# Head-sized TensorE tiles for the attention products of a two-layer convolution kernel, with the scaling on ScalarE

## The chip, the core and the metric

The kernel runs on one core of one Trainium2 chip, in one launch. The metric is the device time of the whole launch in microseconds (us). Shares and stages below come from one profiled execution of the kernel before the change.

## What is computed

The input holds 32 images of 1024 channels and 14 x 14 = 196 positions, in 32-bit floats. Layer 0 is a chain of three table look-ups by soft assignment, with normalisations between them; the change does not touch it. Layer 1 is a linear attention with 16 heads of 64 channels and a depthwise 3 x 3 convolution beside it:

```python
q = elu(Wq @ x[:, :512] + bq) + 1          # 1024 features per position
k = elu(Wk @ x[:, 512:] + bk) + 1
q_rope, k_rope = rope(q), rope(k)          # rotation of feature pairs
z = 1 / (einsum('bhdn,bhd->bhn', q, mean_n(k)) + 1e-6)
kv = (1 / n) * einsum('bhdn,bhen->bhde', k_rope, v)   # v = x, by heads, n = 196
out = einsum('bhdn,bhde->bhne', q_rope, kv) * z
x = x + out + depthwise3x3(x)              # x inside is group-normalised
```

Each head has its own 64 x 64 matrix `kv`. Products of one head's keys with another head's values are not part of the result.

## The kernel before, in words

The launch has two parts. Layer 0 fills the first 2310 us or so. Layer 1 follows; it takes the images two at a time, in 16 pairs, and `pair(p, t)` writes down the work of pair `p`.

In layer 1 nothing is issued in program order. Every piece of work is handed to `do(engine, rank, weight, fn, reads, writes, ...)`. `Plan.write()` then runs a small simulation with the pieces' weights (microseconds) as durations and the ranks as priorities, and issues the pieces of each engine in the order in which the simulation starts them. So each engine's instruction order is fixed when the kernel is built, and an engine that waits for one piece does not take the next one. The ranks of pair `p` are those of the table `due`, shifted by 80 per pair, so that work of neighbouring pairs interleaves.

The work of one pair, by the names and lines that matter below:

- **Front** (`front`, L1623 to L1642): finishes layer 0 for this pair; ScalarE scales (L1623), VectorE adds and takes statistics (L1632, L1637, L1642). `group_norm` averages them with small TensorE products (L1679) and ends on GpSimd. `normalise` (L1736) writes the normalised image `y` with a margin, and a scaled copy `x`.
- **Projections** (`channels`, L1770 to L1791): 16 pieces, each of four 128 x 128 x 392 TensorE products into a bank of the ring `mm`, then two ScalarE steps (L1779, L1782) and one VectorE step (L1787 for queries, L1791 for keys).
- **Rotation** (`rope`, L1814, L1815): on GpSimd.
- **Token-major copies** (`tokens`, L1832, L1835): TensorE transposes four blocks into an `mm` bank, ScalarE copies them out into `vt` (values) or `kt` (keys). The positions of an image are cut in two halves of 105.
- **Key-value products** (`products`, L1856 to L1895): four pieces per pair, one for each image `i` and each half `jp` of the features. A piece has 16 matmuls (two feature tiles `j`, real and imaginary part `r`, two position halves `h`, two column halves `hp`). One of them has 105 rows, 64 weight columns and 128 moving columns, so it covers two heads' keys against two heads' values, and half of what it computes belongs to no head. VectorE's `blocks` (L1878) multiplies the 128 x 512 result by the mask `bmask`, which zeroes the foreign blocks and holds the factor 1/196 too, and writes the tile `kv`.
- **Normalisers** (`normalisers`, L1902 to L1930): 16 matmuls of 128 rows and 32 weight columns, each feature tile into its own 32 output partitions (L1920), then a VectorE reciprocal (L1930). `normalise_q` (L1955) multiplies the rotated queries on GpSimd.
- **Query products** (`attend`, L1974): four pieces per pair, one per feature tile. A piece has eight matmuls (two images, `r`, two halves `hp` of the rows) of 64 rows and 128 weight columns; rows 0 to 63 go to the PSUM bank `pa[0]`, rows 64 to 127 to the bank `pa[1]`.
- **Convolution** (`lepe`, L1992): VectorE adds seven or eight of the nine taps onto the `pa` banks, one instruction per tap, and adds the sum to `x` (L2006). Further taps go over ScalarE and GpSimd (`side_tap`, L2021, L2029). In the last pair three of four feature tiles have their taps as diagonal matmuls on TensorE instead (L2048).

PSUM is shared out as four `mm` banks, three `pa` banks and one bank `w`. A bank of `mm` is taken by any of the projections, transposes, products and normalisers, and is free again when its reader is done. There is one `kv` tile for each `i` and `jp`, so that a pair's result can be written only after the query products of the pair before have read theirs.

`tables` makes the mask once, with two VectorE instructions (L476, L477), during layer 0. A multiplication of 32-bit numbers shows as two TensorE passes in the trace: every matmul leaves two matmul records and two weight-load records.

Of the kernel before, what the change touches and what calls it, by code (L numbers as in the profile page):

```python
# [11 lines left out]
AF = mybir.ActivationFunctionType  # L12
ALU = mybir.AluOpType
# [4 lines left out]
P = 128  # L18
C = 1024
CT = C // P  # L20
HW = 196
# [11 lines left out]
def bc(ap, axis, n):  # L33

    u = ap.unsqueeze(axis)
    shape = list(u.shape)
    shape[axis] = n
    return u.to_broadcast(shape)
# [12 lines left out]
class Plan:  # L51
# [13 lines left out]
    def do(self, engine, rank, weight, fn, reads=(), writes=(), port=False, lag=0.12):  # L65
        n = len(self.pieces)
        before = set()
        for k in reads:
            before |= {self.last[k]} if k in self.last else set()
            self.read.setdefault(k, []).append(n)  # L70
        for k in writes:
            before |= set(self.read.pop(k, []))
            before |= {self.last[k]} if k in self.last else set()
            self.last[k] = n
        slots = []
        for k in (*reads, *writes):
            s = k[0] if isinstance(k, tuple) else k
            if isinstance(s, Slot) and s not in slots:
                slots.append(s)
                s.left += 1  # L80
        self.pieces.append((engine, rank, weight, fn, before - {n}, slots, port, lag))
# [68 lines left out]
def conv_preact_kernel(ctx: ExitStack, tc: tile.TileContext, a: dict, out: bass.AP):  # L150
    nc = tc.nc
# [272 lines left out]
    given = {}  # L424

    def attention_inputs(stack):

        def loads(_):  # L430
            pool = stack.enter_context(tc.tile_pool(name="pre", bufs=1, side="right"))

            def tile_(name, shape):
                given[name] = pool.tile(shape, F32, tag=name, name=name)
                return given[name]

            for n, k in (("qb", a["qb"]), ("kb", a["kb"].rearrange("o (r j p) -> p (o r) j", p=P, r=2))):
                nc.sync.dma_start(tile_(n, [P, 2, 4]), k)
                tile_(n + "u", [P, 2, 4])
                tile_(n + "d", [P, 2, 4])  # L440
            for n, shape in (("lepe_w", [P, CT, 9]), ("lepe_b", [P, CT]), ("kvmask", [P, 256])):
                nc.sync.dma_start(tile_(n, shape), a[n])

            for n in ("cosq", "sinq"):
                t = tile_(n, [P, 4, 14])
                v = a[n].rearrange("p j (r c) -> p j r c", c=14)
                nc.sync.dma_start(t[:, :2], v[:, :2, :, 0])
                nc.sync.dma_start(t[:, 2:], v[:, 2:, 0, :])
            for n, shape in (
                ("hmean", [P, 4]),  # L450
                ("bmask", [P, P]),
                ("hp", [P, 4, 32]),
                ("hsel", [P, P]),
                ("x1", [P, 4, N2]),
                ("x0", [P, 4, N2]),
                ("o3_0", [P, 2, N2]),
                ("o3_1", [P, 2, N2]),
            ):
                tile_(n, shape)
            for h in (1, 0):  # L460
                for i in range(2):
                    nc.sync.dma_start(
                        given[f"x{h}"][:, :, i * HW : (i + 1) * HW],
                        x[i, 4 * h * P : 4 * (h + 1) * P].rearrange("(c q) n -> q c n", q=P),
                    )

        def tables(scratch):
            g = given

            for n in ("qb", "kb"):  # L470
                nc.vector.tensor_scalar(g[n + "u"], g[n], 1.0, None, ALU.add)
                nc.vector.tensor_scalar(g[n + "d"], g[n], -1.0, None, ALU.mult)

            hmask = g["kvmask"].rearrange("p (h e) -> p h e", e=64)[:, :, 0]
            nc.vector.tensor_scalar(g["hmean"], hmask, 1.0 / HW, None, ALU.mult)
            nc.vector.tensor_tensor(g["bmask"], g["kvmask"][:, :P], g["kvmask"][:, P:], ALU.add)  # L476
            nc.vector.tensor_scalar(g["bmask"], g["bmask"], 1.0 / HW, None, ALU.mult)  # L477

            nc.vector.memset(g["hp"], 0.0)
            nc.vector.tensor_copy(g["hp"][:, :, :4], bc(hmask, 1, 4))  # L480

        def heads(scratch):
            g = given
            ph = scratch(P)
            nc.tensor.transpose(ph, g["hp"].rearrange("p j h -> p (j h)"), ident)
            nc.vector.tensor_copy(g["hsel"], ph)

        def third(_):
            for k in range(2):
                nc.sync.dma_start(given[f"o3_{k}"], o3d[:, 4 + 2 * k : 6 + 2 * k, :N2])  # L490

        def projection(b):
            t = a["wkT" if b < 4 else "wqT"]
            return lambda: load_lut(b, t[(b % 4) * P : (b % 4 + 1) * P])

        return [loads, third, tables, heads], [projection(b) for b in range(8)], [third]


# [977 lines left out]
    with ExitStack() as s:  # L1476
# [5 lines left out]

        wk, wq = weights[:4], weights[4:]
        bias = {n: (given[n + "u"], given[n + "d"]) for n in ("qb", "kb")}
        lw, lb, hmean, bmask, sel, cos, sin = (
            given[n] for n in ("lepe_w", "lepe_b", "hmean", "bmask", "hsel", "cosq", "sinq")
        )


# [6 lines left out]
        for k in range(2):  # L1496
            t = once.tile([P, CT, LY], F32, tag=f"y{k}", name=f"y{k}")
            v = t[:, :, LEAD : LEAD + 2 * IMG]
# [21 lines left out]
        for j in range(4):  # L1520
            t = once.tile([P, 2, 2, 2, TP], F32, tag=f"kr{j}", name=f"kr{j}")
# [14 lines left out]
        def ring(name, n, shape, pool=None, tag=None):  # L1536
            tiles[name] = [
                (pool or p2).tile(shape, F32, tag=tag or f"{name}_{k}", name=f"{name}_{k}")
                for k in range(n)
            ]  # L1540
# [11 lines left out]
            ring(f"kt{h}", 1, [TP, 2, 512])  # L1552
        for i in range(2):
            for jp in range(2):
                ring(f"kv{i}{jp}", 1, [P, 2, 2, P])
        for n, k in (("mm", 4), ("pa", 3), ("w", 1)):
            ring(n, k, [P, 512], mm)
        plan = Plan(tiles)
        do = plan.do
# [296 lines left out]
        def products(i, jp, kts, vts, rank):  # L1856

            pk = Slot("mm")
            t = Slot(f"kv{i}{jp}")

            def piece():
                pv = pk().rearrange("p (j r e) -> p j r e", j=2, r=2)
                for j in range(2):
                    for r in range(2):
                        for h in range(2):
                            for hp in range(2):
                                c = 2 * (2 * jp + j) + hp
                                k0 = (2 * j + r) * P + 64 * hp
                                nc.tensor.matmul(  # L1869
                                    pv[64 * hp : 64 * hp + 64, j, r],  # L1870
                                    kts[h]()[:, jp, k0 : k0 + 64],
                                    vts[h]()[:, c * P : (c + 1) * P],
                                    start=(h == 0),
                                    stop=(h == 1),
                                )

            def blocks():
                nc.vector.tensor_tensor(  # L1878
                    t().rearrange("p j r e -> p (j r) e"),
                    pk().rearrange("p (j e) -> p j e", e=P),  # L1880
                    bc(bmask, 1, 4),
                    ALU.mult,
                )

            do(
                PE,
                rank,
                1.97,
                piece,
                [(kt, jp) for kt in kts] + [(vt, jp) for vt in vts],  # L1890
                [pk],
                lag=0.25,
            )
            do(DVE, rank - 10, 0.61, blocks, [pk], [t])
            return t  # L1895

        def normalisers(p, qs, ks, rank):
# [66 lines left out]
        def attend(j, kvs, qr, pa, rank, onto):  # L1964

            def piece():
                for i in range(2):
                    for r in range(2):  # L1970
                        for hp in range(2):
                            v = slice(64 * hp, 64 * hp + 64)
                            n = 210 - 14 * i
                            nc.tensor.matmul(  # L1974
                                pa[hp]()[:, i * 210 : i * 210 + n],
                                kvs[i, j // 2]()[v, j % 2, r],
                                qr()[v, r, i * HW : i * HW + n],
                                start=(r == 0 and not onto),
                                stop=(r == 1 and (i == 1 or not onto)),
                            )  # L1980

            do(PE, rank, 1.57, piece, [kvs[0, j // 2], kvs[1, j // 2], qr], pa, lag=0.25)
# [277 lines left out]
```

## Time and profile before

| what | value |
|---|---|
| median of 3 runs | 3439.27 us (3438.05 to 3441.15) |
| profiled execution, its own time | 3446.09 us |
| its span in the trace | 3444.3 us |
| granted TensorE clock over the span | 0.99 |
| matmul records, busy time | 19217, 3368.4 us |
| VectorE busy, ScalarE busy, GpSimd busy | 2938.9, 1671.0, 2538.4 us |
| key-value products (L1869) | 2048 records, first 2368.3 us, last 3406.3 us |
| query products (L1974) | 1024 records, first 2398.2 us |

The profiled execution is 6.8 us longer than the median. In the profile, PE is the matmul side of TensorE and PEld its weight loads, DVE is VectorE, ACT ScalarE, POOL GpSimd, SP the engine that issues DMAs. "out<-in" names the tiles of a group of instructions. Durations of neighbouring instructions overlap a little, matmuls most of all, so the cost of a piece is read from its start to the start of the next one.

### The profile page before, as it was taken

The numbers are of one execution on the slowest core, as the hardware profiler recorded it, in microseconds if no ns is written. First come the engines' busy times: TensorE is split into PE (matmuls) and PEld (weight loads), VectorE is DVE, ScalarE is ACT, GpSimd is POOL, SyncE is SP. The second block draws the span as 40 slices with busy tenths as digits, with TensorE's granted clock in tenths as the row PEclk, the third lists the DMA queues.
The fourth block names the chain that finished last, engine by engine and source line by source line (L and its number), as shares of the span: only waits on it lengthen the run. The fifth ranks groups of instructions, "written<-read, shape, count | busy, mean of one in ns | idle before, by whom it ended". The sixth has DMA issues, their size and how long they took to land. (4 is left out here: it accounts for less than half of the span.)

```text
span 3444.3 us, 54933 instructions
## 1 busy us (share of the span) xinstructions
PE 3368.4 (98%) x19217; PEld 2088.5 (61%) x19217; DVE 2938.9 (85%) x4621; ACT 1671.0 (49%) x3843; POOL 2538.4 (74%) x1558
## 2 busy tenths in 40 slices
PE   8999999998999999999999999979999999999999
PEld 4555555554455445545488888866666666666665
DVE  7999999997888888888576666646999999999996
ACT  4555555554444434443311111118676767676765
POOL 5999999996888988898322222218888888888887
PEclk9999999999999999999999999989999999999999
DMA  3110111103434444443131111131233332333221
GB/s 117 46 48 28 46 46 47 30 24 113 134 109 128 123 114 109 127 123 98 33 91 38 49 49 49 47 130 41 69 90 87 87 87 81 87 87 91 79 76 48
DMA packets 242229, 267.44 MB, mean 78 GB/s; under 512 B 32812, under 2 KB 239700, under 8 KB 241944
## 3 DMA queue, kind: packets, MB, share of 16 engines
q1 hardware_dynamic: 241248, 263.52, 26.3%
q8 instruction: 155, 2.54, 0.3%
q14 instruction: 130, 1.06, 0.1%
q10 hardware_dynamic: 696, 0.31, 0.0%
HBM read 171.01 MB, written 77.09 MB: 72 GB/s over the span
## 5 line engine op out<-in xcount | busy, mean ns | idle before, releaser
L618 POOL TENSOR_TENSOR t<-t,r 128x1568 f32<-128x1568 f32 (+3 forms) x288 | 961.5, 3339 | 531.5 <-issue 201.1
L734 PE MATMUL po<-t,lut 128*128 128x392 f32 x3840 | 1334.6, 500 | 2.5 <-DMA t<-spare 2.5
L734 PEld LDWEIGHTS po<-t,lut 128*128 128x128 f32 x3840 | 711.9, 190 | 603.8 <-issue 83.2
L1770 PE MATMUL mm<-y,lut 128*128 128x392 f32 x2048 | 710.4, 493 | 0.1
L580 DVE STREAM_TRANSPOSE tt<-t 128x1568 f32<-128x1568 f32 (+1 forms) x284 | 517.8, 1823 | 153.4 <-ACT t L568 149.1
L568 ACT ACTIVATE t<-sc,cbias 128x392 f32<-128x392 f32 (+1 forms) x624 | 322.4, 598 | 554.5 <-PE sc L897 191.2
L1992 DVE SCALAR_TENSOR_TENSOR pa<-y,lepe_w,pa 128x406 f32<-128x406 f32 x900 | 537.9, 638 | 3.6 <-PE pa L1974 0.3
L611 DVE STREAM_TRANSPOSE r<-rc 128x1568 f32<-128x1568 f32 (+1 forms) x284 | 520.9, 1834 | 10.4
L1770 PEld LDWEIGHTS mm<-y,lut 128*128 128x128 f32 x2048 | 370.4, 188 | 243.1 <-issue 6.1
L583 POOL TENSOR_TENSOR tt<-tt 128x784 f32<-128x784 f32 x256 | 470.6, 1838 | 30.5 <-DVE tt L580 25.9
L568 ACT ACTIVATE t<-sc,room 128x392 f32<-128x392 f32 x512 | 259.1, 589 | 410.2 <-issue 180.1
L1358 PE MATMUL po<-t,lut 128*128 128x224 f32 (+2 forms) x1352 | 314.8, 416 | 1.3 <-DMA o3d<-o 1.3
L599 DVE TENSOR_REDUCE sm<-tt 128x98 f32<-128x784 f32 (+1 forms) x284 | 293.6, 1034 | 1.1 <-POOL tt L583 0.8
L1358 PEld LDWEIGHTS po<-t,lut 128*128 128x128 f32 (+1 forms) x1352 | 234.7, 190 | 64.5 <-issue 61.8
L601 DVE RECIPROCAL rc<-sm 128x98 f32<-128x98 f32 (+1 forms) x284 | 220.2, 775 | 9.8
L622 ACT ACTIVATE sm<-sm 128x98 f32<-128x98 f32 (+1 forms) x284 | 85.5, 301 | 150.5 <-DVE rc L601 150.5
L1623 ACT ACTIVATE w<-x,tb,gn_a 128x196 f32<-128x196 f32 x248 | 128.3, 517 | 53.8 <-DMA qr<-o3d 29.3
L1814 POOL TENSOR_TENSOR kr<-k,cosq 128x784 f32<-128x784 f32 x64 | 104.3, 1629 | 63.5 <-DVE k L1791 36.7
L1955 POOL TENSOR_TENSOR qr<-qr,zb 128x784 f32<-128x784 f32 x64 | 117.9, 1854 | 39.2 <-DMA zb<-zd 31.5
L1779 ACT ACTIVATE e<-mm,kbd 128x392 f32<-128x392 f32 x128 | 74.5, 582 | 145.4 <-PE mm L1770 145.4
L1782 ACT ACTIVATE e<-e 128x392 f32<-128x392 f32 x256 | 134.9, 527 | 2.1
L1736 ACT ACTIVATE y<-x,gb,ga 128x196 f32<-128x196 f32 x256 | 125.3, 544 | 12.1 <-POOL gb L1699 12.1
(215 smaller groups left out, 4613.1 us busy)
## 6 DMA issues: line engine op xcount, KB each, us to landing
patch<-h1d SPq DMA_DIRECT2D x383, 108.5 KB
x<-in_x_dram SPq DMA_DIRECT2D x32, 784.0 KB
o3d<-o SPq DMA_DIRECT2D x56, 448.0 KB
x<-in_x_dram SPq DMA_DIRECT2D x64, 392.0 KB
out_dram<-x SPq DMA_DIRECT2D x64, 392.0 KB
o<-o3d SPq DMA_DIRECT2D x62, 392.0 KB
h1d<-pad SPq DMA_DIRECT2D x96, 225.0 KB
patch<-h1d SPq DMA_DIRECT2D x383, 54.2 KB
```

Of the source, the lines that this page charges most:

```text
L568: nc.scalar.activation(t[:, j, : sc.shape[1]], sc, AF.Identity if exact else AF.Exp, bias=bias[:, j : j + 1],)
L580: nc.vector.transpose(tt, tf)
L583: nc.gpsimd.tensor_tensor(tv[:, :, :8], tv[:, :, :8], tv[:, :, 8:], ALU.add)
L599: nc.vector.tensor_reduce(sm, tv, AX.X, ALU.add)
L601: nc.vector.reciprocal(rc, sm)
L611: nc.vector.transpose(r, bc(rc, 2, KC))
L618: nc.gpsimd.tensor_tensor(v[:, c], v[:, c], r[:, c], ALU.mult)
L734: nc.tensor.matmul(po[h], luts[b][:, j, h * P : (h + 1) * P], ts[u % len(ts)][:, j, :N2], start=(b == 0 and j == j0), stop=(b == 7 and j = ...
L1358: nc.tensor.matmul(dst, w, x, start=start, stop=stop)
L1770: nc.tensor.matmul(pv(), w[kt][:, m0 : m0 + P], ywin(p, first + kt), start=(kt == 0), stop=(kt == 3),)
L1782: nc.scalar.activation(e(), e(), AF.Exp, scale=-1.0)
L1992: nc.vector.scalar_tensor_tensor(acc, neighbours(p, c, offset(k)), lw[:, c, k : k + 1], acc, ALU.mult, ALU.add,)
```

## The change

The products are cut along the heads. A feature tile of 128 rows holds four heads with 32 rows each (for one `r`), and each head meets 64 value columns.

- `products` issues 32 matmuls of 105 rows, 32 weight columns and 64 moving columns in place of 16 of 105 x 64 x 128. Four neighbouring ones write to the four 32-partition strips of the bank. The result has 256 columns in place of 512 and holds no foreign blocks.
- The mask and its two instructions are gone. `scaled`, one ScalarE instruction over 128 x 256, copies the result out of PSUM with the factor 1/196; it stands in for the VectorE instruction over 128 x 512.
- `attend` issues 16 matmuls of 32 rows and 64 weight columns in place of eight of 64 x 128. The rows of heads 0 and 1 go to partitions 0 to 63 and 64 to 127 of the bank `pa[0]`, those of heads 2 and 3 to the same halves of `pa[1]`.
- The planner's weights change with it: 1.2 in place of 1.97 for a product piece, and 0.42 on ScalarE in place of 0.61 on VectorE. The weight of `attend` stays at 1.57.

```diff
-            nc.vector.tensor_tensor(g["bmask"], g["kvmask"][:, :P], g["kvmask"][:, P:], ALU.add)
-            nc.vector.tensor_scalar(g["bmask"], g["bmask"], 1.0 / HW, None, ALU.mult)
...
-                ring(f"kv{i}{jp}", 1, [P, 2, 2, P])
+                ring(f"kv{i}{jp}", 1, [P, 2, 2, 64])
...
-                pv = pk().rearrange("p (j r e) -> p j r e", j=2, r=2)
+                pv = pk()[:, :256].rearrange("p (j r e) -> p j r e", j=2, r=2)
                 for j in range(2):
                     for r in range(2):
                         for h in range(2):
-                            for hp in range(2):
-                                c = 2 * (2 * jp + j) + hp
-                                k0 = (2 * j + r) * P + 64 * hp
+                            for q in range(4):
+                                c0 = (2 * (2 * jp + j)) * P + 64 * q
+                                k0 = (2 * j + r) * P + 32 * q
                                 nc.tensor.matmul(
-                                    pv[64 * hp : 64 * hp + 64, j, r],
-                                    kts[h]()[:, jp, k0 : k0 + 64],
-                                    vts[h]()[:, c * P : (c + 1) * P],
+                                    pv[32 * q : 32 * q + 32, j, r],
+                                    kts[h]()[:, jp, k0 : k0 + 32],
+                                    vts[h]()[:, c0 : c0 + 64],
                                     start=(h == 0),
                                     stop=(h == 1),
                                 )
 
-            def blocks():
-                nc.vector.tensor_tensor(
-                    t().rearrange("p j r e -> p (j r) e"),
-                    pk().rearrange("p (j e) -> p j e", e=P),
-                    bc(bmask, 1, 4),
-                    ALU.mult,
+            def scaled():
+                nc.scalar.activation(
+                    t().rearrange("p j r e -> p (j r e)"),
+                    pk()[:, :256],
+                    AF.Copy,
+                    scale=1.0 / HW,
                 )
...
-                1.97,
+                1.2,
...
-            do(DVE, rank - 10, 0.61, blocks, [pk], [t])
+            do(ACT, rank - 10, 0.42, scaled, [pk], [t])
...
-                        for hp in range(2):
-                            v = slice(64 * hp, 64 * hp + 64)
+                        for h in range(4):
+                            v = slice(32 * h, 32 * h + 32)
                             n = 210 - 14 * i
+                            e = slice(64 * (h % 2), 64 * (h % 2) + 64)
                             nc.tensor.matmul(
-                                pa[hp]()[:, i * 210 : i * 210 + n],
+                                pa[h // 2]()[e, i * 210 : i * 210 + n],
                                 kvs[i, j // 2]()[v, j % 2, r],
                                 qr()[v, r, i * HW : i * HW + n],
```

More of the change, by code (lines that the diff above doesn't have):

```diff
@@ L450, in loads @@
                 ("hmean", [P, 4]),
-                ("bmask", [P, P]),
                 ("hp", [P, 4, 32]),
@@ L1484, in conv_preact_kernel @@
         bias = {n: (given[n + "u"], given[n + "d"]) for n in ("qb", "kb")}
-        lw, lb, hmean, bmask, sel, cos, sin = (
-            given[n] for n in ("lepe_w", "lepe_b", "hmean", "bmask", "hsel", "cosq", "sinq")
+        lw, lb, hmean, sel, cos, sin = (
+            given[n] for n in ("lepe_w", "lepe_b", "hmean", "hsel", "cosq", "sinq")
         )
```

## The prediction

> **What bounds the kernel now.** I began with the page's busy shares, but they average two layers, and the change lies in the second. So I cut out a stretch there in which the pairs repeat. In the chain of waits the same steps return every 68.4 us; 2429.12 to 3181.90 us holds 11 such periods of 68.43 us. The view of busy time by stretch says of it:
>
> ```profile
> core 0: us, PE busy (x) PEld busy (x) DVE busy (x) ACT busy (x) POOL busy (x), PEclk, DMA share, GB/s
> 2429.12:3181.90 752.78, 745.96 (x4750) 504.56 (x4749) 735.88 (x1762) 525.84 (x1098) 633.04 (x571) 1.00 0.31 85
> ```
>
> PE is idle for 752.78 - 745.96 = 6.82 us, 0.62 us per period. DVE is idle for 16.90 us, 1.54 us per period. So TensorE works 67.8 us of each 68.43 and VectorE 66.9: **two engines are nearly full at once**. ScalarE works 47.8 us and GpSimd 57.5; they have room. A gain needs both PE and DVE to get less work, and this change takes from both.
>
> The chain of waits for one period confirms it. It runs through DVE and ACT for the first part and then along PE without a break:
>
> ```profile
> 2702.90 3.85 DVE pa L1992 x7
> ...
> 2711.78 1.77 ACT x L1736 x4
> ...
> 2718.82 1.17 PE mm L1832 x8
> 2719.98 2.64 PE mm L1770 x8
> 2722.62 1.90 PE mm L1869 x32
> 2724.52 0.61 PE mm L1832 x4
> 2725.13 2.64 PE mm L1770 x8
> 2727.77 1.90 PE mm L1869 x32
> 2729.66 5.47 PE mm L1770 x16
> ```
>
> Two of the pair's four product pieces (L1869) stand on the chain. The timeline of PE shows the other two and the pieces around them; the cost of a piece is the distance from its start to the next start:
>
> ```profile
> 2777.20 3.71 PE L1869 MATMUL mm<-vt,kt 105*64 105x128 f32 x64
> 2780.85 1.53 PE L1920 MATMUL mm<-q,kmm 128*32 128x196 f32 x32
> 2782.31 1.12 PE L1832 MATMUL mm<-ident,kr 128*105 128x128 f32 x8
> 2783.36 1.65 PE L1974 MATMUL pa<-qr,kv 64*128 64x210 f32 x16
> ```
>
> Two products together cost 3.65 us, one alone 1.90 (chain), so products take 2 x 1.90 + 3.65 = 7.45 us per pair. The normalisers cost 1.46 us and a query piece 1.57 (2735.41 to 2736.98 in the same view). The view of one line adds the VectorE step that goes:
>
> ```profile
> L1878 DVE TENSOR_TENSOR kv<-mm,bmask x64: 628/682/693, 2370.4 to 3407.6; 128x512 f32<-128x512 f32 x64
> L476 DVE TENSOR_TENSOR bmask<-kvmask x1: 283/283/283, 1806.5 to 1806.5; 128x128 f32<-128x128 f32 x1
> L477 DVE TENSOR_SCALAR bmask<-bmask x1: 226/226/226, 1806.8 to 1806.8; 128x128 f32<-128x128 f32 x1
> ```
>
> **What the Trainium skill says, and the trace.** (1) "TensorE: Matmul & The Clock Gate", section "The mechanism": matmuls in different tiles of the array run at the same time, with starts about 4 ns apart. The trace agrees on the overlap: in the products two records start 6.7 ns apart and the next two follow 109 ns later; in the normalisers four records start 6.7 ns apart, the next four 166 ns later; in layer 0 (L1027, 27 x 32 tiles) sixteen start within 100 ns. The weight loads of different tiles overlap in the same way. (2) The same page, section "Wait — 56ns, not 53.3ns?": a matmul of N columns costs N / 2.4 GHz + about 2.5 ns. A pass of a 32-bit matmul moves two cycles per column here: 128 x 2 / 2.4 + 2.5 = 109.2 and 196 x 2 / 2.4 + 2.5 = 165.8, and the trace has 109 and 166. The section also gives a floor of about 25 ns between starts of small matmuls; no stretch of this trace comes to it, since the densest sustained one, the normalisers, has 1464 / 32 = 45.8 ns per record. (3) "TensorEngine Tiling (Array Packing)", section "Key Properties": a change of the tiling mode drains the array. A product piece is 16 groups x 109.1 = 1.75 us, and costs 1.90, so such a change costs about 0.15 us. (4) "PSUM — Partial Sum Buffer", section "PSUM bank collisions raise a hardware error": it quotes that different row tiles cannot access one bank at the same time, and reports as measured that only the same bank and the same 32-partition strip collide. The changed `attend` puts two row tiles into two halves of one bank; no row of this trace does that, as each row tile there has a bank of its own.
>
> **The change, part by part, per pair.**
>
> *Products on PE.* 32 matmuls leave 64 records. Four neighbouring ones have four column strips, as in the normalisers, so 16 groups of four. A group streams 64 columns: 64 x 2 / 2.4 + 2.5 = 55.8 ns. Four starts at 6.7 ns need 27 ns, less than that. A load of 32 columns must fit behind a group: two loads of one strip start 28 ns apart in the normalisers. So a piece costs 16 x 55.8 + 0.15 = 1.04 us alone and two together 32 x 55.8 + 0.15 = 1.94: in all 4.02 us, a **saving of 3.43 us**. From below the bound is no drain at all, 0.89 us a piece. From above I take the normalisers' 45.8 ns per record, in case TensorE cannot be fed faster than shown: 64 x 45.8 = 2.93 us, dearer than now by 1.03. I take 1.04, since the sixteen starts of L1027 within 100 ns show that issue itself is quick.
>
> *Query products.* Before, eight groups of two records (four (image, r) steps, two passes); after, eight groups of four. The columns stay at 210 and 196, so the groups stay at 178 and 166 ns, and the cost at 1.57 us. A gain is possible: the first weight load has 64 columns, not 128, worth at most 0.05 us a piece. From above: if two row tiles of one bank take turns, each group streams twice, 8 x 172 = 1.38 us more per piece. I take no change.
>
> *VectorE.* Four L1878 go. From one start to the next they cost 0.60 us, so **2.39 us less**. L476 and L477 lie in layer 0, where PE is full from 1800 to 2200 us; their 0.5 us is worth nothing, and 0.5 us if that cover were gone.
>
> *ScalarE.* Four steps over 128 x 256 from PSUM come in. The copies of 512 columns (L1835) cost 0.47 us from start to start, the 392-column step L1779 0.48; I take 0.46, so 1.84 us more on an engine with 20 us idle per pair. Its own wait is the danger: ScalarE takes its pieces in order, and behind the step stand L1779 and L1782, for which VectorE (L1787, L1791) waits, and the copies L1835, for which PE waits. The planner starts it only when product and `kv` tile are ready in its own time, and the mask has the same waits on VectorE today, so I price it at zero; late by half a product piece four times would be 2 us per pair. No DMA is added or moved; POOL's and SP's instructions stay.
>
> *Order.* The new weights shift the simulated times by 3 of about 70 us and so reorder neighbours. I can't price this from the trace; see the rivals.
>
> **Sum.** PE: 67.81 - 3.43 = 64.4 us of work per pair. DVE: 66.89 - 2.39 = 64.5. They end level. A period of 64.5 plus DVE's present idle of 1.54 is 66.0, a gain of 2.4 us, and PE's idle grows from 0.6 to 1.6. Between the first and the last pair lie 15 periods: 36 us. In the tail the chain runs over two joined products (3.64 us, at 3324.78), worth 1.7 more. So 3446.1 - 37.7 = 3408.4 for an execution like the profiled one, which is 6.8 us above the median: **3401.6**. If DVE's idle shrinks to PE's 0.6, the gain is 3.3 a period, 3388; if it doubles, 0.9 a period, 3424. That is this case's own range.
>
> **The rivals.**
>
> *Row tiles of one bank take turns* (slower). `attend` then costs 1.57 + 1.38 = 2.95 us. PE has 64.4 + 4 x 1.38 = 69.9 us of work, with 0.6 idle 70.5, 2.1 above now: 15 x 2.1, plus 5.5 in the last pair, less 1.7, gives 3474. It decides from 1.57 + 3.43 / 4 = 2.43 us per piece on. For it speaks the quoted rule; against it the measured one on the same page, and row tiles with separate banks that overlap in L1974 and L897.
>
> *TensorE is not fed fast enough.* At the page's 25 ns per record a product piece costs 64 x 25 + 150 ns = 1.75 us, a saving of only 0.15 to 0.3: PE has 67.1 us, the period is 67.8, and the time about 3429. At 45.8 ns PE works 67.8 + 4 x 1.03 = 71.9 and the time is 3500. It turns to a loss above 1.90 us a piece.
>
> *The order eats it.* With ScalarE's step in front of its other work, or neighbours reordered, DVE's idle grows by the 2.4 us freed: 3437, no change. For it speaks that the two engines already wait on each other in turn along the chain; against it, that PE today idles only 0.6 us in the same coupling.
>
> **Chances.** Main case 0.63 (3402); slow feeding at 25 ns 0.09 (3429); order 0.09 (3437, half of it within the bound); turns in a bank 0.11 (3474); feeding at 45.8 ns 0.08 (3500). About 0.2%, 7 us, is what a measurement of this kernel can tell from no change. Faster by more: 0.63 + 0.09 less a little, 0.71; within: 0.09, the rest of main, feeding and order; slower: 0.20. The range runs from 3380, below the main case's best, to 3474, the centre of the next case; about 0.18 is left out.
>
> **What would show it.** L1869 with 4096 records, groups of four 56 ns apart, a lone piece about 1.04 us; L1974 with 2048 records, a piece still 1.57; L1878 gone from VectorE and a ScalarE row of 128 x 256 at about 0.5 us; the period 66.0 us, PE and DVE both idle by about 1.6. A query piece over 2.43 us, or a lone product over 1.90, would prove the forecast wrong on PE; a period of 68.4 with both pieces as forecast would prove the order wrong.

## The result, and the profile after

The changed kernel takes 3404.33 us (median of four runs, 3403.06 to 3404.95) against 3439.22 us before: a ratio of **0.9898**, 95% interval 0.988 to 0.9915, so 34.9 us faster. The forecast was 3401.6 us. The profiled execution took 3404.36 us (span 3402.6), 41.7 us less than the one before; 6.8 us of that is that the earlier one lay above its median.

Busy time by stretch of the changed kernel, over the 11 periods from the second pair's normalisers on:

```profile
core 0: us, PE busy (x) PEld busy (x) DVE busy (x) ACT busy (x) POOL busy (x), PEclk, DMA share, GB/s
2433.63:3157.80 724.17, 709.46 (x6861) 459.97 (x6860) 713.04 (x1715) 538.24 (x1141) 630.61 (x572) 1.00 0.31 89
```

724.17 us for 11 pairs are 65.8 us each, where it was 68.43. PE idles 14.7 us in the stretch (1.3 per pair; before 0.6) and DVE 11.1 (1.0 per pair; before 1.5). Both are still nearly full; there is less for them to do.

The chain of waits of the changed kernel, at the place where the prediction showed two product pieces of 1.90 us:

```profile
2699.55 2.15 PE mm L1829 x16
2701.70 2.70 PE mm L1767 x8
2704.40 1.03 PE mm L1866 x64
2705.43 0.61 PE mm L1829 x4
2706.05 2.64 PE mm L1767 x8
2708.68 1.03 PE mm L1866 x64
2709.71 2.83 PE mm L1767 x8
2712.54 1.53 PE pa L1972 x32
```

The product pieces (now L1866) cost 1.03 us with twice the records, and a query piece (L1972) 1.53 with twice the records. Two joined pieces stand in PE's timeline of the changed kernel:

```profile
2757.72 1.99 PE L1866 MATMUL mm<-vt,kt 105*32 105x64 f32 x128
2759.65 0.68 PE L1829 MATMUL mm<-ident,kr 128*105 128x128 f32 x4
```

From start to start the joined pair costs 1.93 us, where it was 3.65. The view of one line shows the step that took the mask's place:

```profile
L1875 ACT ACTIVATE kv<-mm x64: 359/366/396, 2367.7 to 3369.9; 128x256 f32<-128x256 f32 x64
```

Two things must be known to read the experiments. **Layer 0**, which no kernel here changes, ends (first L1623, in the changed kernel L1620) anywhere between 2296 and 2303 us from one profiled execution to the next. So I read each trace from that first step to the end, called *layer 1* below. And **the planner's order depends on a draw at each build**: it goes through a set of engine names, and the sequence in a set of names changes with each build. It matters in one place: the planner has a lock, `port`, that one engine holds at a time, and VectorE (one small step, L1902) and GpSimd can both want it at the same simulated moment. There are just two possible issue orders, and each trace could be matched, TensorE piece by piece, with one of the two: the kernel before had GpSimd first, the changed kernel VectorE first. The comparison above therefore mixes the change with the draw; the runs e9 and e10 take them apart. The kernel before that ran beside the experiments took 3447 to 3449 us, which fits VectorE first (e10 stands at 0.9999 of it, and e7, with GpSimd first, at 0.998).

| kernel | port first | median us | ratio (interval) | layer 1 us | period us | PE work + idle | DVE work + idle |
|---|---|---|---|---|---|---|---|
| before (first trace) | GpSimd | 3439.2 | 1 | 1142.4 | 68.50 | 67.89 + 0.61 | 66.96 + 1.54 |
| changed (first trace) | VectorE | 3404.3 | 0.9898 (0.988 to 0.9915) | 1103.6 | 66.04 | 64.63 + 1.40 | 64.88 + 1.16 |
| e1, PE relieved alone | GpSimd | 3434.7 | 0.9955 (0.9941 to 0.9968) | 1129.9 | 67.69 | 65.27 + 2.41 | 66.65 + 1.04 |
| e2, DVE relieved alone | VectorE | 3440.9 | 0.9983 (0.9976 to 0.999) | 1142.2 | 68.32 | 67.79 + 0.53 | 65.72 + 2.60 |
| e3, query products alone | GpSimd | 3438.1 | 0.997 (0.996 to 0.9981) | 1139.8 | 68.38 | 67.72 + 0.65 | 66.92 + 1.46 |
| e4, changed, old weights | GpSimd | 3416.9 | 0.9907 (0.9891 to 0.9922) | 1116.9 | 66.73 | 64.33 + 2.39 | 65.14 + 1.59 |
| e5, changed, strip by strip | GpSimd | 3515.3 (one run) | | 1210.1 | 72.77 | 72.31 + 0.46 | 65.35 + 7.42 |
| e6, changed, measured weights | VectorE | 3428.4 | 0.9939 (0.9925 to 0.9952) | 1130.3 | 67.90 | 65.45 + 2.45 | 64.96 + 2.94 |
| e7, before | GpSimd | 3440.7 | 0.9977 (0.997 to 0.9983) | 1141.5 | 68.49 | 67.88 + 0.61 | 66.93 + 1.56 |
| e8, changed | VectorE | 3404.4 | 0.9872 (0.9857 to 0.9887) | 1104.3 | 66.08 | 64.61 + 1.47 | 64.83 + 1.26 |
| e9, changed | GpSimd, fixed | 3412.7 | 0.9894 (0.9879 to 0.9909) | 1112.0 | 66.61 | 64.67 + 1.94 | 64.90 + 1.71 |
| e10, before | VectorE, fixed | 3447.3 | 0.9999 (0.999 to 1.0007) | 1148.1 | 68.65 | 67.67 + 0.98 | 66.64 + 2.01 |
| e11, DVE relieved alone | GpSimd, fixed | 3440.4 | 0.9979 (0.9972 to 0.9986) | 1139.9 | 67.81 | 67.07 + 0.74 | 64.31 + 3.50 |
| e12, changed, other ranks | VectorE, fixed | 3395.9 | 0.9846 (0.9833 to 0.986) | 1096.2 | 65.87 | 64.70 + 1.16 | 64.73 + 1.14 |

The period is the distance between the normalisers of the second and the fifteenth pair, divided by 13; work is the period less the engine's gaps. Work holds short waits inside a piece and slower execution too, so the same matmuls come to anything from 64.3 (e4) to 65.5 us (e6). Ratios from e1 on are to the kernel before that ran beside them.

### The profile page after: what moved, and what is told of

The parts are those of the page before. It is cut to its first block, busy times and chain, and to the rows that moved or that the text cites. A ratio compares the mean times of both kernels' runs of the same rounds, so it can differ in the third digit from the quotient of the medians.

```text
span 3402.6 us, 61025 instructions
## 1 busy us (share of the span) xinstructions
PE 3311.0 (97%) x22289; PEld 2021.4 (59%) x22289; DVE 2906.9 (85%) x4555; ACT 1690.7 (50%) x3907; POOL 2534.4 (74%) x1558
## 5 line engine op out<-in xcount | busy, mean ns | idle before, releaser
L580 POOL TENSOR_TENSOR tt<-tt 128x784 f32<-128x784 f32 x256 | 470.7, 1839 | 31.1 <-DVE tt L577 31.1
L1620 ACT ACTIVATE w<-x,tb,gn_a 128x196 f32<-128x196 f32 x248 | 128.5, 518 | 54.5 <-DVE tb L1488 29.1
L1024 PE MATMUL sc<-patch,room 27*32 27x392 f32 x4096 | 122.9, 505 | 8.3 <-DMA patch<-h1d 8.1
L1355 PE MATMUL po<-x,s 128*128 128x224 f32 x624 | 124.9, 357 | 5.6 <-DVE x L1216 5.6
```

Of the source, the lines that this page charges most:

```text
L580: nc.gpsimd.tensor_tensor(tv[:, :, :8], tv[:, :, :8], tv[:, :, 8:], ALU.add)
L1355: nc.tensor.matmul(dst, w, x, start=start, stop=stop)
```

## The experiments

**e1 and e2: one engine relieved at a time.** e1 has the small matmuls, but VectorE keeps an instruction of the old width:

```diff
-                nc.scalar.activation(t()..., pk()[:, :256], AF.Copy, scale=1.0 / HW)
+                nc.vector.tensor_scalar(t()..., bc(pk()[:, :256], 1, 2), 1.0 / HW, None, ALU.mult)
...
-            do(ACT, rank - 10, 0.42, scaled, [pk], [t])
+            do(DVE, rank - 10, 0.61, scaled, [pk], [t])
```

> The changed matmuls, but the scaling stays on VectorE with an instruction as wide as the old one (it writes the 256 columns twice, 512 in all), so only TensorE gets less work. Theory (two engines are full, both must be relieved): PE work about 64.4 us per pair, DVE work 66.9, so the period is 66.9 plus 1.0 to 1.5 us of idle, 67.9 to 68.4, and the time 3430 to 3439. Rival 1 (TensorE alone is the bound): nearly the whole gain, 3404 to 3412. Rival 2 (VectorE alone is the bound): no gain, 3439, and the next run has it all.

e2 has the old 16 matmuls and no mask; the finer query products read only their own blocks:

```diff
-                    pk()[:, :256],
+                    pk(),
...
-            do(ACT, rank - 10, 0.42, scaled, [pk], [t])
+            do(ACT, rank - 10, 0.49, scaled, [pk], [t])
...
-                                kvs[i, j // 2]()[v, j % 2, r],
+                                kvs[i, j // 2]()[v, j % 2, r, e],
```

> The old 16 product matmuls of 105x64x128, but no mask: ScalarE scales all 512 columns, and the changed query products read only their own blocks. So only VectorE gets less work. Theory: PE work 67.7 us per pair plus 0.6 of idle, so the period stays at 68.2 to 68.4, and the time at 3433 to 3439. Rival 1 (TensorE alone is the bound): the same, 3437. Rival 2 (VectorE alone is the bound): the whole gain, about 3404.

Both rivals fall: neither engine alone brings the gain. e1 came to 3434.7 us, as the theory had it (its period of 67.69 is 0.2 below the range); e2's period is 68.32 as expected, and its time of 3440.9 is 2 us above. Since e2 was built with the other draw than e1, it was run again with the draw of e1 and of the kernel before:

> The kernel with only VectorE relieved (old 16 product matmuls, no mask, scaling on ScalarE, changed query products), with GpSimd first, the draw of the kernel before and of the kernel with only TensorE relieved (its earlier run had VectorE first). Theory (PE stays full at 67.8 us per pair): period 68.2 to 68.8, 1138 to 1146 us from the first front step to the end. Rival (VectorE's relief brings a gain of its own, which the other draw hid): a period of 67.5 or less.

Layer 1 took 1139.9 us, as expected. The period of 67.81 is outside the expectation, but only because the second pair came late and the third early; from the fourth pair to the fifteenth it is 68.34. So with GpSimd first throughout, layer 1 is 1141.5 (e7), PE relieved 1129.9, DVE relieved 1139.9, both 1112.0 (e9): gains of 11.6 and 1.6 us alone, and **29.5 us together, over twice their sum**. Each of these kernels has an issue order of its own, and an order alone can move layer 1 by more than that surplus (1104.3 us in e8, 1130.3 in e6, with the same work), so the factor is rough. Where the freed time went does not depend on it. Busy time by stretch, over the same 710 us of each, shows how. The kernel before (e7):

```profile
core 0: us, PE busy (x) PEld busy (x) DVE busy (x) ACT busy (x) POOL busy (x), PEclk, DMA share, GB/s
2450.00:3160.00 710.00, 704.30 (x4456) 475.80 (x4453) 693.19 (x1667) 493.69 (x1033) 598.75 (x541) 1.00 0.31 86
```

PE relieved alone (e1):

```profile
2450.00:3160.00 710.00, 684.86 (x6405) 441.77 (x6404) 698.38 (x1668) 506.51 (x1046) 602.09 (x547) 1.00 0.30 86
```

VectorE relieved alone (e11):

```profile
2450.00:3160.00 710.00, 701.63 (x5113) 464.93 (x5108) 671.95 (x1624) 515.95 (x1074) 598.46 (x542) 1.00 0.30 87
```

Both relieved (e9):

```profile
2450.00:3160.00 710.00, 692.00 (x6550) 446.97 (x6552) 691.89 (x1675) 523.87 (x1104) 615.31 (x561) 1.00 0.30 89
```

In e1 PE's idle grows from 5.7 us to 25.1, and DVE is fuller than ever (11.6 idle). In e11 it is the reverse: PE 8.4, DVE 38.0. The time freed on one engine is spent waiting for the other. In e9 both idle 18 us, and the same 710 us hold more pairs (GpSimd's busy time, the same per pair in all, rises from 599 to 615 us).

**e3: the query products alone**, in the kernel before:

```diff
-                        for hp in range(2):
-                            v = slice(64 * hp, 64 * hp + 64)
+                        for h in range(4):
+                            v = slice(32 * h, 32 * h + 32)
...
+                            e = slice(64 * (h % 2), 64 * (h % 2) + 64)
-                                pa[hp]()[:, i * 210 : i * 210 + n],
-                                kvs[i, j // 2]()[v, j % 2, r],
+                                pa[h // 2]()[e, i * 210 : i * 210 + n],
+                                kvs[i, j // 2]()[v, j % 2, r, e],
```

> The kernel before with the changed query products alone (16 matmuls of 32 rows x 64 columns, reading their blocks of the masked 128-column tile). Theory: a query piece costs 1.53 us in place of 1.57, 0.16 us per pair on PE, so at most 2.6 us in all: 3436 to 3440. Rival (the finer query tiles themselves bring the gain, for example by freeing the pa banks earlier): 3425 or less. Rival (row tiles of one bank disturb each other only in some pieces): 3445 or more.

Layer 1 fell from 1141.5 (e7) to 1139.8 us: 1.7 us, near the 2.6 that 64 pieces of 0.04 us can give, and both rivals fall. The ratio of 0.997 is mostly the draw: e7, with nothing changed, has 0.9977.

**e4 and e6: the same work in other orders.** e4 gives the planner the old weights (1.97 and 0.61):

> The changed kernel with the planner's old weights (1.97 for a product piece; 0.61 for the scaling, on ScalarE), so that the same work is issued in nearly the old order. Theory (the gain is the engines' work, the order matters little): 3400 to 3412. Rival (the gain, or a good part of it, comes from the new order): 3420 or more.

e6 gives it what the trace shows:

```diff
-            do(PE, rank, 2.76, product, ...)
+            do(PE, rank, 2.64, product, ...)
...
-            do(PE, rank, 2.3, piece, [*qk, ("kmm", 0), ("kmm", 1)], [pd], lag=0.25)
+            do(PE, rank, 1.46, piece, [*qk, ("kmm", 0), ("kmm", 1)], [pd], lag=0.25)
```

(and 0.44 for a token copy, 1.03 for a product piece, 1.53 for a query piece, 0.27 for the scaling)

> The changed kernel with the planner's weights set to what the trace shows from start to start: projection 2.64 (2.76), token copy 0.44 (0.5), product 1.03 (1.2), normalisers 1.46 (2.3), query piece 1.53 (1.57), ScalarE's scaling 0.27 (0.42). The work stays the same. Theory (the old-weights run showed that the issue order is worth 0.7 us per pair): the period moves by up to 0.7 us either way, 3393 to 3415; the floor is the work of 64.6 us per pair, that is 3384. Rival (the order no longer matters once both engines are level): 3402 to 3407.

e4 was a miss by 5 us: 3416.9. But it was built with GpSimd first, and beside e9, the changed kernel with that draw (66.61), its period of 66.73 is the same to 0.12 us; its layer 1 is 4.9 us longer. The old weights cost little. e6 was a miss on both sides, 3428.4: weights nearer to the truth made a period of 67.9, 1.8 worse than e8 with the same draw. Waits of PE in e6:

```profile
PE pa L1972 <- DVE x L2004: 7.9, 8, 2.4
PE mm L1829 <- ACT kt L1832: 7.0, 7, 2.2
```

and in the changed kernel, over as long a stretch:

```profile
PE mm L1829 <- ACT kt L1832: 3.0, 5, 0.9
PE mm L1767 <- DVE k L1788: 1.8, 2, 1.2
PE pa L1972 <- DVE x L2004: 1.8, 3, 0.9
```

In e6 a query piece stands at the head of PE's queue before VectorE has freed its bank (L2004), for up to 2.4 us at a time, and transposes wait longer for ScalarE. I read this as the planner taking TensorE to be ahead of where it is when its weights hold no reserve; which of the six weights does it was not tried.

The waits cost more than their own length. Of the 1.82 us per pair between e8 and e6, PE's idle is 0.98; the other 0.84 is PE's work, and the instructions are the same. Two lots of eight matmuls in e6's timeline, and its busy time from 2673.8 us on:

```profile
2672.80 4.59 PE L1767 MATMUL mm<-y,lut 128*128 128x392 f32 x8 [2.01 <-ACT vt L1832]
2679.38 2.80 PE L1767 MATMUL mm<-y,lut 128*128 128x392 f32 x8
2673.80:2677.20 3.40, 3.40 (x6) 1.35 (x4) 2.97 (x4) 2.09 (x5) 3.40 (x4) 0.50 0.02 5
```

After a wait of 2.01 us the eight matmuls took 4.59 us in place of 2.80, and the granted clock (third number from the end) stood at 0.50. In e6's 13 periods there are five such stretches, 23.8 us in all, each starting within 4.0 us after the start of a PE wait of 2.0 to 3.7 us. In e8's there is none, and no PE wait over 1.35 us. PE is busy for 21.7 us of the 23.8; half of that, lost to the halved clock, is 10.9 us or 0.83 per pair, which accounts for the extra work. So nearly half of e6's loss is the clock. That the long waits bring the low clock is what the traces suggest, not a rule: a wait of 2.1 us in e1 was not followed by one.

**e5: neighbours in the same strip.**

```diff
-                for j in range(2):
-                    for r in range(2):
-                        for h in range(2):
-                            for q in range(4):
+                for q in range(4):
+                    for j in range(2):
+                        for r in range(2):
+                            for h in range(2):
```

> The changed kernel with the 32 matmuls of a product piece in another order: all eight of one 32-partition strip, then the next strip, so that neighbours no longer lie in different tiles of the array. Theory (the saving is the overlap of four neighbouring tiles): the 64 records follow each other at 55.8 ns in part or in full; without any overlap a piece costs 64 x 55.8 = 3.6 us, with two strips at once 1.8 us; PE then has 3 to 10 us more work per pair, and the time is 3440 to 3560. Rival (TensorE finds matmuls of free tiles further down its queue, or a piece was bound by something else): a piece still costs 1.03 us and the time is that of the changed kernel.

PE's timeline of e5:

```profile
2817.84 3.16 PE L1866 MATMUL mm<-vt,kt 105*32 105x64 f32 x64
2820.93 0.69 PE L1829 MATMUL mm<-ident,y 128*105 128x128 f32 x4
2824.31 3.18 PE L1866 MATMUL mm<-vt,kt 105*32 105x64 f32 x64
```

The same 64 records cost 3.1 us, three times as much, and the kernel 3515 us, slower than before the change. Single records show 55.8 ns from start to start inside a strip, and two at once for about eight records at each change of strip. So the saving is the overlap of neighbours in four strips, and TensorE does not reach far enough down its queue to find them elsewhere.

**e7 to e10: the draw.** The kernel before and the changed one, measured again as they are:

> The kernel before, unchanged, measured like an experiment. Theory (differences of up to 7 us between kernels on this chip come from layer 0, which none of them changes, and not from layer 1): its ratio to the kernel before lies within 0.998 to 1.002, and from the first L1623 to the end it takes 1142 us as in its first trace. Rival (layer 1 itself varies from one execution to the next): that stretch differs by over 3 us.

> The changed kernel, unchanged, measured beside the others. Theory: from the first front step to the end 1103 to 1105 us as in its first trace, a ratio of 0.987 to 0.992. Rival (part of the gain was the luck of one chip or one execution): that stretch is over 1108 us, or the ratio above 0.993.

Layer 1 repeats to 0.9 and 0.7 us. But e7's ratio was 0.9977, just outside what I expected, and that set me looking for the draw. With it fixed in one line:

```diff
-        engines = {p[0] for p in self.pieces}
+        engines = ("PE", "ACT", "POOL", "DVE", "SP")
```

> The changed kernel with one line of the planner fixed: where VectorE and GpSimd could both take the shared port at the same simulated moment, GpSimd is asked first. The planner of all kernels so far went through a set of engine names, whose sequence is drawn anew with every build: the traces show that the kernel before was built with GpSimd first, the changed kernel with VectorE first, so the comparison mixes the change with that draw. Theory (the engines' work makes the gain; the draw is worth under 1 us per pair either way): period 65.5 to 67.0 us, and 1095 to 1115 us from the first front step to the end, against 1142 for the kernel before with the same draw. Rival (the draw made the gain): a period over 67.5, and 1130 or more.

(e10: VectorE and GpSimd exchanged in that line, in the kernel before)

> The kernel before with the same line fixed the other way, VectorE first, which is the draw that the changed kernel had. Theory: PE's work of 67.9 us per pair stands, so the period is 68.3 to 69.5 and the stretch from the first front step to the end 1138 to 1160 us. Rival (the draw made the gain): a period of 67 or less and 1120 or less.

Both theories held. With GpSimd first the change takes 1141.5 to 1112.0 us in layer 1, 29.5 less (medians 3440.7 to 3412.7); with VectorE first 1148.1 to 1104.3, 43.8 less (3447.3 to 3404.4). **The change gains with either draw, 28 to 43 us by the medians**; in layer 1 the draw moves the kernel before by 6.6 us and the changed one by 7.7, in opposite directions. The measured 34.9 us is one of four possible pairings.

**e12: a better order for the same work.**

```diff
-    def do(..., port=False, lag=0.12):
+    def do(..., port=False, lag=0.2):
...
-                do(DVE, rank - 20, 0.86, greater, ...)
+                do(DVE, rank - 20, 0.7, greater, ...)
...
-            den=45,
+            den=50.0,
-            attend=75.5,
+            attend=71.5,
-            lepe=98,
+            lepe=94.0,
```

(with the draw fixed to VectorE first, and 1.5 for the normalisers and for a query piece)

> The changed kernel with the same work and another issue order: VectorE asked first (fixed), the query products, the convolution taps earlier by 4 ranks, the normalisers later by 5, and five planner values nearer to the trace (key step 0.70, normalisers 1.5, query piece 1.5, a hand-over of 0.20 between engines). Theory (PE works 64.6 and DVE 64.9 us per pair, the rest of the 66.0 us period is waiting that an order can take away): the period falls to between 65.0 and 66.0 us, and from the first front step to the end it takes 1080 to 1103 us, against 1104 for the changed kernel. Rival (such weights make the order worse, as the measured weights did at 67.9): 1110 us or more.

It took 3395.9 us, the lowest of all kernels here, with period and layer 1 as the theory had them. Layer 1 is 8.1 us shorter than e8's: 2.7 us of that over the 13 periods, 3.3 before the second pair's normalisers, 2.0 after the fifteenth's. Its trace still has two stretches at half clock, 10.2 us in all, after PE waits of 1.8 and 1.9 us. Which of the changed values brings the gain was not tried.

## Why the prediction was right, point by point

- **Products on PE**: forecast 1.04 us alone and 1.94 joined, measured 1.03 and 1.93. Single records show groups of four 6 to 7 ns apart, and groups 56 ns apart, as worked out, with two cycles per column, from the formula of the Trainium skill ("TensorE: Matmul & The Clock Gate", section "Wait — 56ns, not 53.3ns?"). The rival of slow feeding is refuted: the records follow at 1030 / 64 = 16 ns each, and at 15 ns through 128 of them. The page's floor of 25 ns does not hold across tiles. The trace before could have said so for short runs: at 903 us, 32 records of L1027 start within 0.46 us, 15 ns each, so the prediction's reading that no stretch of it comes to the floor was wrong, and that rival was given too much.
- **PE's work in all** fell by 3.26 us per pair (67.89 to 64.63), less than the 3.49 that the product pieces alone gave up (7.44 to 3.95; forecast 3.43). The four query pieces rose from 6.37 to 6.51 and the projections from 42.88 to 43.03 (all counted from start to start less gaps, over the 13 periods). In the one query piece followed record by record (2760.26 to 2762.37, 2.11 us), a pause of 0.36 us comes after the first four records; what it waits for was not traced.
- **Query products**: forecast 1.57 with up to 0.05 less, measured 1.53 where no wait falls into the piece. The rival of row tiles taking turns in one bank is refuted: four records start 7 ns apart and the next four 178 ns later. The page "PSUM — Partial Sum Buffer" ("PSUM bank collisions raise a hardware error") quotes the rule that different row tiles cannot access one bank at the same time, and reports as measured, for accesses by two engines, that different 32-partition quadrants of one bank run clean. In this trace two row tiles write to different halves of one bank and do not slow each other, so the quoted rule does not hold here.
- **VectorE**: forecast 2.39 us less work per pair; the work went from 66.96 to 64.88, 2.08 less. The mask's step went as forecast, but another step, overlooked, grew. It is the one VectorE step under the planner's lock `port`, before and after:

```profile
L1902 DVE TENSOR_TENSOR kmm<-ks,hmean x32: 166/180/1203, 2368.2 to 3410.0; 128x32 f32<-128x32 f32 x32
L1899 DVE TENSOR_TENSOR kmm<-ks,hmean x32: 168/318/2764, 2346.1 to 3341.7; 128x32 f32<-128x32 f32 x32
```

Over the 13 periods it is busy for 4.62 us before and 11.65 after, 0.54 us more per pair. All 16 of its records over 400 ns in the changed kernel end 46 to 52 ns after a GpSimd instruction ends (before, all four such records, 45 to 50 ns). So I read the long ones as held up behind GpSimd: the lock keeps the two apart only in the planner's own time. No run tested it.
- **ScalarE**: forecast 0.46 us a step, measured 0.26 from start to start. This was mis-sized, because I took the cost of wider rows nearly whole; it lies beside other work and cost nothing either way. PE waited on the new step for 1.1 us in 11 periods.
- **The period**: forecast 66.0 us, measured 66.04. PE's idle rose to 1.40 (forecast 1.6), DVE's fell to 1.16 (forecast 1.54). That both must be relieved for the whole gain is shown by e1, e2 and e11. That the number fits so closely is luck: DVE's work came out 0.4 us above the forecast's 64.5 and its idle 0.4 below. The idle was carried over from the kernel before, not derived; with the same work it is 1.1 to 2.9 us in e4, e6, e8, e9 and e12.
- **The sum**: forecast 37.7 us less for the profiled execution; it was 41.7 us, 38.8 in layer 1 and 3.0 in layer 0, which the change does not touch. Of the 38.8 the 13 periods give 32.0 (forecast 31.1), the start 1.2 and the tail 5.6; these two ends hold one more period each, and the forecast for both is 6.5. Here too luck helped: with the same draw in both kernels layer 1 gains 29.5 or 43.8 us, and the forecast's 37.7 lies between. Subtracting the 6.8 us between profile and median again gave 3401.6; the changed kernel's profiled execution equals its median, and so the medians differ by 2.8 us less than I summed.
- **The order** was the weak step: priced at nothing, and given 0.09 as a rival. The same work took periods of 66.1 to 67.9 us (e8, e9, e4, e6), and 65.9 in e12. In e6 it ate 1.8 of the 2.4 us that the sum promised, nearly half of that through the clock. The forecast hit 66.0 with a good order; with the draw of the kernel before it would have been 66.6, still inside the main case's own range.

## What to carry to other kernels

Where two engines are both nearly full, price a change on each and take the period from the larger remainder; relieving one alone turns into waiting on the other. Matmuls that fill a fraction of the array pay only if neighbours in program order lie in different tiles (e5). Look at the granted clock of the stretch, not of the whole run, before a longer busy time is put down to the work: e6's mean was 0.99. Before comparing two builds of a kernel whose order is planned at build time, make the order the same each time: here an unordered set alone was worth about 7 us in either kernel.

## What the runs showed of the hardware that I had not expected

- TensorE sustains a matmul record and a weight load every 15 ns (128 of each in 1.93 us) when four neighbours lie in four strips; with neighbours in one strip it is 55.8 ns, and only about eight records around each change of strip overlap.
- The scaling copy on ScalarE out of PSUM costs 0.264 us from start to start over 128 x 256, and 0.478 over 128 x 512 (e11). Between these two that is about 0.05 us fixed and 0.84 ns per column, well below the 0.46 us that I had taken for the narrow one.
- After PE waits of about 2 us and more the granted clock fell to 0.50 for 3.4 or 6.8 us at a time in e6 (five times in the 13 periods), though not after every such wait in every run.
- A VectorE multiply over 128 x 32, normally 0.18 us, lasted up to 2.76 us in the changed kernel, and all 16 records over 0.4 us ended about 50 ns after a GpSimd instruction did.
